# Two banded mixing layers: which engine scales two of the eight columns of the second norm, and which copies the band's products

## The chip, the cores and the metric

The kernel runs on one core of one Trainium2 chip. The core has five engines that run side by side, each through its own list of instructions in order: TensorE (PE in the profile; its weight loads are PEld), VectorE (DVE), ScalarE (ACT), GpSimd (POOL) and SyncE (SP), which here issues the loop's transfers. The metric is the time of one execution on the device in microseconds (us).

## The reference

The input x is 512 x 512 x 64 in float32. Two layers follow one another, each `x = x + layer(gn(x))`, with this body (H = 128, window 4):

```
xn    = ln(gn(x))                                     # 64 channels
left  = (xn @ Wl + bl) * mask * sigmoid(xn @ Wlg + blg)   # 128 channels
right = (xn @ Wr + br) * mask * sigmoid(xn @ Wrg + brg)
gate  = sigmoid(xn @ Wog + bog)
band[i, j, :] = sum over |d| <= 4 of left[i + d, i, :] * right[i + d, j, :]
out   = (ln(band) * out_norm_scale + out_norm_bias) * gate
y     = out @ Wo + bo                                 # back to 64 channels
```

`ln` takes mean and variance over the channels of one position. The second norm, the one meant in the title, is `ln(band)`: 128 channels per position.

## The kernel before

Rows of x come in 9 blocks of 64 rows that overlap by the window, and the columns in two halves that lie on the partitions: partition e*64 + i is row i of the block, half e. Half a row, 256 columns, is worked through in 2 chunks of 128 columns, each in 16 units of 8 columns. That makes 9 x 2 x 16 = 288 units per layer, and as many outputs.

The loop in `layer` runs over steps t. One step works on one unit coming in and, some 30 steps behind it, on one output going out:

- In: `scaled` and `moved` (the affine of the group norm, z times ga plus gb), `inner_stats`, `centred`, `rescaled` (the first norm), `transposed`, `kept` (the transposed unit, zT, also written to the DRAM tensor `later`), `right` (the projections, into two PSUM banks), `right_gate` (sigmoid, sg), `right_end` (the product into RO). The four elementwise steps on z run on GpSimd, apart from the first units of each layer, which VectorE scales and moves.
- Between: `mix` multiplies a slab of the left factors, A, with RO: the band's products for 8 channels and a whole chunk, in two PSUM banks. Two copies, "copy a" and "copy b", put them back into RO in place of the right factors. Each chunk has 16 such products, spread over ten of its 16 steps as 2, 1, 2, 2, 1, 2, 1, 2, 2, 1, and none in the other six.
- Out: `out_stats` (statistics of RO, sto), `norm` (the second norm of the 8 columns of one output, one instruction per column, from RO into the tile `on`), `turned` (transposes of `on`), `gates` and `gated`, `times_gate` (ZH), `end` (the product with Wo), `ended` (the addition to x, in XR) and, in the first layer, `sums` and `biased`.

Every fourth step, `solve` computes the reciprocal roots for both norms at once: `prepare` on ScalarE ("solve on a") and thirteen small instructions on VectorE, `roots` ("solve on d"). They leave rs and nm, the factor and the offset of each column.

What stands where is written out by hand: FIRST and SECOND list the parts of one step for the two layers, and each engine gets its instructions in the order of that list. `keep_in_program_order` (line 381) holds every instruction of the loop to it, so nearly all rows of the profile name that line, and the tile names tell them apart. The tile `on` has one buffer: the columns of the next output are written only when `turned` has read this one.

Of the 8 columns of an output, GpSimd scales the last `nv` ("norm columns"; 1 in the first layer, 2 in the second) and ScalarE the others, columns 0 to 3 early in the step and the rest at its end. `copy a` is ScalarE's. `copy b` is VectorE's, apart from the second product of a step in the first layer, which is ScalarE's.

Of the kernel before, what the change touches and what calls it, by code (L numbers as in the profile page):

```python
# [10 lines left out]
AF = mybir.ActivationFunctionType  # L11
ALU = mybir.AluOpType
# [10 lines left out]
JU = 8  # L23
# [9 lines left out]

APART = (False, True)
NV = (1, 2)
SECOND_ON_ACT = (True, False)

FIRST = [
    ("out stats", 2), "gates", "gated", ("project", 0), ("project", 4), "turn",
    ("sigmoid", 0), ("out stats", 3), "scale", ("right", 0), ("sigmoid", 4),  # L40
    ("norm", (0, 4)), "norm columns", "centre", "move", "last product", ("right", 4),
    "times gate", "rescale", "transpose", ("out stats", 99), "inner stats", "keep", "solve",
    "end", ("band", 0), ("copy a", 0), "sums", "bias", ("band", 1), ("copy b", 0),
    ("solve on", "a"), "scale next", "move next", ("norm", (4, 8)), ("copy a", 1),
    ("solve on", "d"), ("copy b", 1),
]
# [2 lines left out]
    ("sigmoid", 0), ("project", 4), ("out stats", 99), ("right", 0), ("sigmoid", 4), "turn",  # L49
    ("norm", (0, 4)), "last product", "norm columns", "centre", "scale next", "rescale",  # L50
    "times gate", "transpose", ("band", 0), "keep", "move next", "end", ("right", 4),
    ("copy b", 0), "inner stats", "solve", "move", ("copy a", 0), ("band", 1),
    ("solve on", "a"), ("copy b", 1), ("copy a", 1), ("norm", (4, 8)), ("solve on", "d"),
]
ORDERS = (FIRST, SECOND)
# [48 lines left out]
def tile_two_banded_layers(  # L104
# [9 lines left out]
    x, out = x[0], out[0]  # L114
# [268 lines left out]
    class en:  # L383
        tensor, vector, scalar, gpsimd, sync = map(
            InOrder, (nc.tensor, nc.vector, nc.scalar, nc.gpsimd, nc.sync)
        )
# [285 lines left out]

        return {"a": [prepare], "d": [roots]}

    def norm(o: Out, lo: int, hi: int, pool: bool):
        if lo == 0:
            o.on = onp.tile([P, JU, H], F32, tag="on", name="on")
        for j in range(lo, hi):
            to, of = o.on[:, j, :].rearrange("p (h t) -> p h t", t=2), RO[:, :, o.c + j, :]
            rs, nm = o.rs[:, j : j + 1], o.nm[:, j : j + 1]  # L680
            if pool:
                en.gpsimd.tensor_scalar(to, of, rs, nm, ALU.mult, ALU.add)
            else:
                en.scalar.activation(to, of, AF.Identity, bias=nm, scale=rs)

    def recall(o: Out):
        o.t = ztg.tile([P, JU // 2, P], F32, tag="zg", name="zg")
# [96 lines left out]
    def layer(src: bass.AP, dst: bass.AP, w: dict, stats: bool, then=None):  # L784
# [4 lines left out]
        units, outs, lefts, mixes, looks, slabs = {}, {}, {}, {}, {}, {}  # L789
# [4 lines left out]
        for c in range(n_chunks):  # L794
            b, t0 = blocks[c // per], (c + 1) * NU
            for k in range(NU):
                t = c * NU + k
# [4 lines left out]
            for f in range(NU):  # L802
                o = outs[c * NU + LAG + f] = Out(
                    b, units[c * NU + (f + own) % NU], c % per * JC + f * JU
                )
# [10 lines left out]
        for n in range(0, NEAR * JQ, JU):  # L816
            t = 3 + n // JU * 2
# [24 lines left out]
            load(src, u)  # L842
        yield
        A, sti, sto = {}, {}, None
        order, nv, second_on_act = (x[0 if stats else 1] for x in (ORDERS, NV, SECOND_ON_ACT))
        for t in range(min(loads), last_t + 3):
            if then and t == max(units) + 2:
                then()
            if t + 3 in outs:
                recall(outs[t + 3])  # L850
            for u in loads.get(t, []):
                if u not in early:
                    load(src, u)
            if t + 1 in outs:
                fetch(src, outs[t + 1], w, t + 1)
            for c, h in slabs.get(t, []):
                A[c, h] = take_left(c // per, h)

            looking = []
            for o, k in looks.get(t, []):  # L860
                if sto is None:
                    sto = sm.tile([P, NB // 2, 6], F32, tag="sto", name="sto"), []
                st, os = sto
                if k == 0:
                    os.append(o)
                n = (len(os) - 1) * (JU // 2)
                looking.append((o, st[:, n : n + JU // 2, :], k))
            todo = []
            for at, u in inners.get(t, []):
                key = (at + 1) // 4  # L870
                if key not in sti:
                    sti[key] = sm.tile([P, 3 * NB // 4, 6], F32, tag="sti", name="sti", bufs=3), []
                st, us = sti[key]
                n = len(us) * (JU // 2)
                u.mean = st[:, n : n + JU // 2, 1::3]
                todo += [(u, st[:, n : n + JU // 2, :], k) for k in range(JU // 2)]
                us.append(u)
            mixing, mixed, solving = mixes.get(t, []), [], {}
            now, later_on = affines.pop(t, []), []
            if t % 4 == 0 and t > NU:  # L880
                later_on = affines.pop(t + 1, [])
            if t in lefts:
                for q in range(0, min(JU, NEAR * JQ - lefts[t].near), JQ):
                    left(lefts[t], q, w)
            which = lambda u: en.vector if u.at < NU + 4 else en.gpsimd

            for item in order:
                name, n = item if isinstance(item, tuple) else (item, None)
                u, o, p = units.get(t), outs.get(t), outs.get(t - 1)
                if name == "out stats":  # L890
                    for v in looking[:n]:
                        out_stats(*v)
                    looking = looking[n:]
                elif name == "scale":
                    for v in now:
                        scaled(v, which(v))
                elif name == "move":
                    for v in now:
                        moved(v, which(v))
                elif name == "scale next":  # L900
                    for v in later_on:
                        scaled(v, en.gpsimd)
                elif name == "move next":
                    for v in later_on:
                        moved(v, en.gpsimd)
                elif name == "project" and u:
                    right(u, n, w)
                elif name == "sigmoid" and u:
                    right_gate(u, n)
                elif name == "right" and u:  # L910
                    right_end(u, n)
                elif name == "gates" and o:
                    gates(o, w)
                elif name == "gated" and o:
                    gated(o)
                elif name == "turn" and o:
                    turned(o, w)
                elif name == "times gate" and o:
                    times_gate(o, w)
                elif name == "centre":  # L920
                    for v in inputs(t + 2):
                        centred(v)
                elif name == "rescale":
                    for v in inputs(t + 2):
                        rescaled(v)
                elif name == "transpose":
                    for v in inputs(t + 1):
                        transposed(v)
                elif name == "keep":
                    for v in inputs(t + 1):  # L930
                        kept(v)
                elif name == "bias" and o:
                    biased(o, w)
                elif name == "inner stats":
                    for v in todo:
                        inner_stats(*v)
                elif name == "last product" and p:
                    end(p, w)
                elif name == "end" and p:
                    ended(dst, p)  # L940
                elif name == "sums" and t - 2 in outs:
                    sums(outs[t - 2], t - 2 == first_t, t - 2 == last_t)
                elif name == "solve" and t % 4 == 0:
                    st, us = sti.pop((t + 4) // 4, (None, []))
                    so, os = sto or (None, [])
                    sto = None
                    if us or os:
                        solving = solve(w, us, os, st, so)
                elif name == "solve on":
                    for f in solving.pop(n, []):  # L950
                        f()
                elif name == "norm" and t + 1 in outs:
                    lo, hi = n
                    norm(outs[t + 1], lo, min(hi, JU - nv), False)
                elif name == "norm columns" and t + 1 in outs:
                    norm(outs[t + 1], JU - nv, JU, True)
                elif name == "band" and len(mixing) > n:
                    c, h0 = mixing[n]
                    mixed.append(mix(c, A[c, h0 // HA], h0, stats))
                elif name == "copy a" and len(mixing) > n:  # L960
                    en.scalar.copy(*mixed[n][0])
                elif name == "copy b" and len(mixing) > n:
                    (en.scalar.copy if n and second_on_act else en.vector.tensor_copy)(*mixed[n][1])

    class Slices:

# [143 lines left out]
```

## Time and profile before

| | |
|---|---|
| time, median of 3 runs | 4660.42 us (4649.69 to 4669.49) |
| span of the profiled execution, first to last instruction | 4644.6 us |
| TensorE busy | 3860.9 us, 83% of the span |
| VectorE busy | 3999.6 us, 86% |
| ScalarE busy | 3596.2 us, 77% |
| GpSimd busy | 3278.3 us, 71% |
| the second norm's columns on ScalarE | 3744 instructions, 492 ns each |
| the same on GpSimd | 864 instructions, 451 ns each |

The page gives the profiled execution's span; the time of a run lies a little above a span, 16 us here between the median and this one. The first layer's loop runs from about 260 us to 2470 us, the second's from there to the end, so the shares of the span are means over two loops, their beginnings and ends, and the statistics of the input ahead of them. A busy TensorE is not TensorE at its peak. In a row of grouped instructions, the first number behind the bar is the time that at least one of them ran, the next the mean length of one; instructions of an engine overlap a little, so the first may be less than number times length. Behind the second bar stands the idle time just before them and what ended it.

### The profile page before, as it was taken

To read this page: it belongs to the slowest core of one execution; us is meant where nothing else is said; L and a number is where in the kernel's file an instruction comes from. 1 tells how busy PE (TensorE), PEld (TensorE's weight loads), DVE (VectorE), ACT (ScalarE), POOL (GpSimd) and SP (SyncE) were. 2 spreads that over 40 slices of the span, in tenths; PEclk is the share of its full clock that TensorE was granted. 3 is DMA by queue.
4 is the path that set the end of the run, shared out by engine and by line. 5 is a ranking of instruction groups with operands and counts; after the bars stand their busy time and mean duration, and the time that the engine had idled before them with its cause. 6 is when DMAs were issued, how large, how long until landed. Compare 5 with 4: busy or idle time off the path is not lost. (4 is left out here: it accounts for less than half of the span.)

```text
span 4644.6 us, 192669 instructions
## 1 busy us (share of the span) xinstructions
PE 3860.9 (83%) x76306; PEld 3310.7 (71%) x76306; DVE 3999.6 (86%) x10943; ACT 3596.2 (77%) x8410; POOL 3278.3 (71%) x3427
## 2 busy tenths in 40 slices
PE   1024899999999999999984389899999898899998
PEld 0023788888888888888863378777777787778776
DVE  7954798898899989899876379999999999999998
ACT  0012799999999999999983268888888888888888
POOL 0034888888888888888733387877778777778751
PEclk9986999999999999999997699999999999999999
DMA  7949678777878777888763968888888888888876
GB/s 309 394 134 99 177 218 221 218 218 219 222 220 222 217 219 217 225 220 224 211 184 95 72 191 219 222 223 224 221 227 221 226 226 225 222 222 223 227 210 184
DMA packets 1437803, 983.43 MB, mean 212 GB/s; under 512 B 167362, under 2 KB 1284584, under 8 KB 1432552
## 3 DMA queue, kind: packets, MB, share of 16 engines
q1 hardware_dynamic: 1432064, 969.69, 77.1%
q8 instruction: 603, 9.88, 0.9%
q14 instruction: 296, 2.42, 0.2%
q10 hardware_dynamic: 4840, 1.43, 0.1%
HBM read 658.35 MB, written 312.40 MB: 209 GB/s over the span
## 5 line engine op out<-in xcount | busy, mean ns | idle before, releaser
L381 ACT ACTIVATE on<-RO,nm,rs 128x128 f32<-128x128 f32 x3744 | 1589.4, 492 | 87.7 <-DVE nm L381 50.8
L381 PEld LDWEIGHTS banks<-pack,zT 64*128 64x128 f32 x18576 | 1270.1, 197 | 467.4 <-ACT zT L381 324.5
L381 PE MATMUL banks<-pack,zT 64*128 64x128 f32 x18576 | 1326.1, 287 | 262.2 <-ACT zT L381 234.8
L381 DVE TENSOR_TENSOR RO<-banks,sg 128x512 f32<-128x512 f32 (+1 forms) x1188 | 794.6, 676 | 306.9 <-ACT sg L381 206.1
L381 ACT ACTIVATE sg<-banks 128x512 f32<-128x512 f32 (+1 forms) x1188 | 694.1, 591 | 254.9 <-PE banks L381 227.3
L381 POOL TENSOR_TENSOR z<-z,ga 128x512 f32<-128x512 f32 x536 | 682.0, 1281 | 184.5 <-DMA z<-mid_x 169.5
L381 DVE BATCH_NORM_STATS2 sto<-RO 128x6 f32<-128x256 f32 x2304 | 803.3, 412 | 0.8
L381 POOL TENSOR_SCALAR on<-RO,rs,nm 128x128 f32<-128x128 f32 x864 | 384.2, 451 | 566.3 <-ACT sg L381 309.8
L381 DVE SCALAR_TENSOR_TENSOR ZH<-bank,pack,gate 128x448 f32<-128x448 f32 (+1 forms) x1152 | 739.1, 683 | 43.7 <-ACT gate L381 24.8
L381 PE MATMUL bank<-zg,pack 64*128 64x448 f32 (+1 forms) x2304 | 724.8, 595 | 19.0 <-ACT RO L381 8.3
L381 PE MATMUL bank<-pack,ZH 128*64 128x64 f32 x18432 | 669.4, 226 | 21.4 <-DVE nm L381 20.5
L381 POOL TENSOR_TENSOR z<-z,gb 128x512 f32<-128x512 f32 x536 | 678.0, 1278 | 5.1
L381 POOL TENSOR_TENSOR z<-z,rs 128x512 f32<-128x512 f32 x586 | 618.5, 1056 | 72.3 <-DVE rs L381 45.4
L381 POOL TENSOR_TENSOR z<-z,sti 128x512 f32<-128x512 f32 x586 | 624.9, 1067 | 21.4 <-DVE sti L381 21.4
L381 PEld LDWEIGHTS bank<-pack,ZH 128*64 128x64 f32 x18432 | 589.6, 139 | 64.6 <-DVE nm L381 27.5
L381 ACT ACTIVATE zT<-banks 128x512 f32<-128x512 f32 (+1 forms) x1084 | 461.9, 477 | 146.0 <-DMA later<-zT 75.3
L381 ACT ACTIVATE gate<-bank 128x448 f32<-128x448 f32 (+1 forms) x1152 | 562.5, 540 | 5.8 <-PE bank L381 2.7
L381 DVE BATCH_NORM_STATS2 sti<-z 128x6 f32<-128x128 f32 x2344 | 503.7, 282 | 1.4 <-POOL z L381 1.2
L381 PE MATMUL bank<-ident,on 64*128 64x64 f32 x9216 | 459.5, 226 | 31.1 <-ACT gate L381 28.3
L381 PEld LDWEIGHTS bank<-ident,on 64*128 64x128 f32 x9216 | 429.3, 141 | 74.9 <-ACT gate L381 50.2
L381 DVE TENSOR_TENSOR XR<-bank,XR 120x512 f32<-120x512 f32 (+1 forms) x576 | 390.9, 679 | 5.2 <-POOL XR L381 2.3
L381 PE MATMUL banks<-ident,z 64*128 64x64 f32 x4336 | 251.1, 234 | 131.2 <-DVE RO L381 68.7
(154 smaller groups left out, 4025.2 us busy)
## 6 DMA issues: line engine op xcount, KB each, us to landing
later<-zT SPq DMA_DIRECT2D x576, 256.0 KB
A<-left_of SPq DMA_DIRECT2D x1152, 128.0 KB
zg<-later SPq DMA_DIRECT2D x576, 256.0 KB
z<-in_x_dram SPq DMA_DIRECT2D x576, 128.0 KB
z<-mid_x SPq DMA_DIRECT2D x576, 128.0 KB
gn_x<-in_x_dram SPq DMA_DIRECT2D x16, 4096.0 KB
XR<-in_x_dram SPq DMA_DIRECT2D x448, 112.0 KB
mid_x<-XR SPq DMA_DIRECT2D x448, 112.0 KB
```

The lines of the kernel that those rows point to most:

```text
L381: return lambda *a, **k: tc.keep_in_program_order(f(*a, **k))
```

## The change

Columns 8 - nv - 2 and the one after it are scaled on VectorE, as one `tensor_scalar` each, in a new part of the step called "norm vector". ScalarE keeps 5 of the 8 columns in the first layer and 4 in the second; GpSimd keeps its own. All copies of the band's products are on ScalarE, and in the second layer "copy b" of the first product moves in the list from ahead of the inner statistics to behind "copy a".

```
+DVE_NORM = 2
 FIRST = [
...
-    "end", ("band", 0), ("copy a", 0), "sums", "bias", ("band", 1), ("copy b", 0),
+    "end", ("band", 0), ("copy a", 0), "sums", "norm vector", "bias", ("band", 1),
+    ("copy b", 0),
...
 SECOND = [
...
-    ("copy b", 0), "inner stats", "solve", "move", ("copy a", 0), ("band", 1),
+    "inner stats", "norm vector", "solve", "move", ("copy a", 0), ("copy b", 0), ("band", 1),
...
-            if pool:
-                en.gpsimd.tensor_scalar(to, of, rs, nm, ALU.mult, ALU.add)
+            if engine is en.scalar:
+                engine.activation(to, of, AF.Identity, bias=nm, scale=rs)
             else:
-                en.scalar.activation(to, of, AF.Identity, bias=nm, scale=rs)
+                engine.tensor_scalar(to, of, rs, nm, ALU.mult, ALU.add)
...
-                    norm(outs[t + 1], lo, min(hi, JU - nv), False)
+                    norm(outs[t + 1], lo, min(hi, JU - nv - DVE_NORM), en.scalar)
...
+                elif name == "norm vector" and t + 1 in outs:
+                    norm(outs[t + 1], JU - nv - DVE_NORM, JU - nv, en.vector)
...
-                    (en.scalar.copy if n and second_on_act else en.vector.tensor_copy)(*mixed[n][1])
+                    en.scalar.copy(*mixed[n][1])
```

The lists of TensorE, GpSimd and SyncE stay as they are; only VectorE's and ScalarE's change. VectorE's list in the middle of the first layer, a step with one product of the band, before (sti and sto are the statistics of the two norms):

```order
L381 BN_STATS sti<-z 128x6 x4
L381 TENSOR_TENSOR XR_977<-bank,XR_977 120x4x128
L381 COPY RO<-banks 128x2x256
L381 BN_STATS sto<-RO 128x6 x4
L381 TENSOR_TENSOR RO<-banks,sg 128x64x8 x2
```

The same step with the change:

```order
L382 BN_STATS sti<-z 128x6 x4
L382 TENSOR_TENSOR XR_977<-bank,XR_977 120x4x128
L382 TENSOR_SCALAR on<-RO,rs,nm 128x128 x2
L382 BN_STATS sto<-RO 128x6 x4
L382 TENSOR_TENSOR RO<-banks,sg 128x64x8 x2
```

The copy out of the PSUM banks is gone, and two columns of the norm stand in its place, in steps without a product too.

ScalarE's list in the second layer, a solving step with two products of the band, before (var and the two rows behind it are `prepare`):

```order
L381 ACTIVATE zT<-banks 128x4x64
L381 COPY RO<-bank 128x2x256
L381 ACTIVATE var<-sti,ln_eps 128x32
L381 COPY bank<-sto 128x32
L381 ACTIVATE bank<-sto 128x32
L381 COPY RO<-bank 128x2x256
L381 ACTIVATE on<-RO,nm,rs 128x128 x2
L381 ACTIVATE gate<-bank 128x448 x2
```

The same step with the change:

```order
L382 ACTIVATE zT<-banks 128x4x64
L382 COPY RO<-bank 128x2x256 x2
L382 ACTIVATE var<-sti,ln_eps 128x32
L382 COPY bank<-sto 128x32
L382 ACTIVATE bank<-sto 128x32
L382 COPY RO<-bank 128x2x256 x2
L382 ACTIVATE gate<-bank 128x448 x2
```

`prepare` now stands behind two copies of the first product instead of one, two copies follow it instead of one, and the two late columns of the norm are gone from ScalarE.

More of the change, by code (lines that the diff above doesn't have):

```diff
@@ L35 @@
 NV = (1, 2)
-SECOND_ON_ACT = (True, False)
+DVE_NORM = 2
 FIRST = [
@@ L673, in solve, with norm @@
         return {"a": [prepare], "d": [roots]}
-    def norm(o: Out, lo: int, hi: int, pool: bool):
+    def norm(o: Out, lo: int, hi: int, engine):
         if lo == 0:
@@ L844, in layer @@
         A, sti, sto = {}, {}, None
-        order, nv, second_on_act = (x[0 if stats else 1] for x in (ORDERS, NV, SECOND_ON_ACT))
+        order, nv = (x[0 if stats else 1] for x in (ORDERS, NV))
         for t in range(min(loads), last_t + 3):
@@ L953, in layer @@
                     lo, hi = n
-                    norm(outs[t + 1], lo, min(hi, JU - nv), False)
+                    norm(outs[t + 1], lo, min(hi, JU - nv - DVE_NORM), en.scalar)
                 elif name == "norm columns" and t + 1 in outs:
-                    norm(outs[t + 1], JU - nv, JU, True)
+                    norm(outs[t + 1], JU - nv, JU, en.gpsimd)
+                elif name == "norm vector" and t + 1 in outs:
+                    norm(outs[t + 1], JU - nv - DVE_NORM, JU - nv, en.vector)
                 elif name == "band" and len(mixing) > n:
```

## The prediction

> **What bounds the kernel now.** I read the busy time by stretch first, for the steady middle of each layer; columns after the window's length are PE, PEld, DVE, ACT and POOL busy us.
>
> ```profile
> 929.00:2322.00 1393.00, 1344.33 (x28011) 1169.66 (x28006) 1254.61 (x3402) 1290.14 (x3035) 1204.85 (x1186) 1.00 0.80 220
> 2786.00:4528.00 1742.00, 1585.42 (x31584) 1369.81 (x31580) 1636.27 (x4436) 1509.08 (x3503) 1343.83 (x1502) 0.98 0.81 223
> ```
>
> To turn these into steps I took the groups of instructions of the same two stretches, the first layer's here: one GpSimd column per step, so 201 steps of 1393/201 = 6.93 us.
>
> ```profile
> L381 ACT ACTIVATE on<-RO,nm,rs 128x128 f32<-128x128 f32 x1409 | 596.9, 492 | 13.9 <-DVE nm L381 11.2 <-POOL z L381 1.4 <-ACT sg L381 0.5
> L381 POOL TENSOR_SCALAR on<-RO,rs,nm 128x128 f32<-128x128 f32 x201 | 90.6, 451 | 135.6 <-ACT sg L381 89.3 <-PE bank L381 44.6
> L381 DVE COPY RO<-banks 128x512 f32<-128x512 f32 x124 | 84.6, 683 | 0.7 <-ACT RO L381 0.7
> ```
>
> In the second layer two GpSimd columns per step, so 256 steps of 1742/256 = 6.80 us:
>
> ```profile
> L381 DVE BATCH_NORM_STATS2 sto<-RO 128x6 f32<-128x256 f32 x1024 | 355.2, 411 | 0.1
> L381 POOL TENSOR_SCALAR on<-RO,rs,nm 128x128 f32<-128x128 f32 x512 | 226.2, 452 | 215.5 <-ACT sg L381 186.0 <-PE bank L381 27.4
> L381 DVE BATCH_NORM_STATS2 sti<-z 128x6 f32<-128x128 f32 x988 | 212.0, 282 | 1.4 <-POOL z L381 1.2
> L381 DVE COPY RO<-bank 128x512 f32<-128x512 f32 x257 | 175.4, 682 | 10.0 <-PE bank L381 8.8
> L381 ACT COPY RO<-bank 128x512 f32<-128x512 f32 x257 | 150.1, 585 | 39.2 <-PE bank L381 37.7
> ```
>
> Per step that is, in us: first layer PE 6.69, ACT 6.42, DVE 1254.61/201 = 6.24, POOL 5.99; second layer DVE 1636.27/256 = 6.39, PE 6.19, ACT 5.89, POOL 5.25. Four engines are nearly full. In the first layer PE leads at 97% with DVE at 90%; in the second DVE leads at 94%. So an extra half microsecond of DVE work per step cannot be hidden in either layer. The waits of the second layer show the rest of its step:
>
> ```profile
> POOL z L381 <- DMA z<-mid_x: 162.5, 47, 6.1
> PEld banks L381 <- ACT zT L381: 138.7, 96, 5.3
> DVE bank L381 <- ACT bank L381: 37.5, 17, 4.9
> ```
>
> Some is data arriving late (162.5 us); the third row is DVE waiting for ScalarE's preparation of the reciprocal roots.
>
> **The change, part by part.**
>
> ScalarE loses two columns per step, 2 x 596.9/1409 = 0.85 us. It gains the copies that VectorE made: 124/201 = 0.62 per step in the first layer and one per step in the second, at 150.1/257 = 0.58 us. Net -0.49 and -0.26 us per step. ScalarE does not lead in either layer, so I give this no gain of its own; its cover is DVE.
>
> VectorE loses the same copies: 84.6/201 = -0.42 us per step in the first layer, 175.4/256 = -0.69 in the second. It gains two columns per step, 128 elements from RO in SBUF to `on` in SBUF with two per-partition scalars. No such VectorE instruction runs in the loop now. The nearest rows are in the set-up, SBUF to SBUF with one per-partition scalar:
>
> ```profile
> L247 DVE TENSOR_SCALAR aug<-raw,ns 128x640 f32<-128x640 f32 x2 | 1.1, 544 | 17.2 <-DMA nb<-in_L_conv_norm_bias_dram 17.2
> L245 DVE TENSOR_SCALAR hb<-half,nb 128x128 f32<-128x128 f32 x2 | 0.6, 278 | 0.0
> ```
>
> So 0.278 us each by the row of the same size. As instructions overlap their neighbours' ends, the floor is the 128-element statistics, 212.0/988 = 0.215 us each. I take 0.50 us for the pair. Were that all, DVE would go to 6.24 + 0.50 - 0.42 = 6.32 and 6.39 + 0.50 - 0.69 = 6.20: even, and slightly lighter.
>
> It is not all. The two set-up rows differ by 512 elements and 266 ns, 0.52 ns an element; the two statistics rows differ by 128 elements and 129 ns, 1.01 ns an element. VectorE's SBUF-to-SBUF scalar operation therefore takes two elements at a time and must read SBUF over two paths. What happens when VectorE reads SBUF over two paths while GpSimd works is in this trace, at the start of the second layer, where VectorE does some units' affine step itself (z and ga or gb both in SBUF). Undisturbed, then beside GpSimd (columns: start us, length us):
>
> ```profile
> 2499.58 1.28 DVE L381 TENSOR_TENSOR z<-z,ga 128x512 f32<-128x512 f32 x2
> 2620.24 0.95 DVE L381 TENSOR_TENSOR z<-z,gb 128x512 f32<-128x512 f32 x1
> 2621.11 1.52 DVE L381 TENSOR_TENSOR z<-z,ga 128x512 f32<-128x512 f32 x1
> 2619.59 1.05 POOL L381 TENSOR_TENSOR z<-z,sti 128x512 f32<-128x512 f32 x1
> 2620.72 1.37 POOL L381 TENSOR_TENSOR z<-z,rs 128x512 f32<-128x512 f32 x1
> ```
>
> Alone, two take 1.28 us, 0.6 to 0.7 each. Beside GpSimd the first ends at 2621.19, 0.55 us after GpSimd's ends at 2620.64; GpSimd's next is stretched from its usual 1.05 to 1.37 us behind it; and VectorE's second, issued at once, ends at 2622.63, 0.54 us after that one's end at 2622.09. They take strict turns, whole instruction by whole instruction, and a second VectorE instruction has to let a waiting GpSimd instruction pass. The other VectorE work of the loop reads one operand from PSUM or has only one; the new pair would be the loop's first to collide.
>
> Where the pair stands, GpSimd is in the middle of its list. One step of the first layer, where the pair would follow the XR row:
>
> ```profile
> 1512.14 0.68 DVE L381 TENSOR_TENSOR XR<-bank,XR 120x512 f32<-120x512 f32 x1
> 1512.73 1.72 DVE L381 BATCH_NORM_STATS2 sto<-RO 128x6 f32<-128x256 f32 x5
> 1512.10 1.04 POOL L381 TENSOR_TENSOR z<-z,rs 128x512 f32<-128x512 f32 x1
> 1513.10 1.18 POOL L381 TENSOR_TENSOR XR<-XR,fewer 120x512 f32<-120x512 f32 x1
> ```
>
> The first column would wait from 1512.8 to 1513.14, the second until after the 1.18 us behind it. On average: GpSimd's share is 1204.85/1393 = 0.865 with 1204.85/1186 = 1.02 us an instruction, and 1343.83/1742 = 0.771 with 1343.83/1502 = 0.89. The first of the pair waits share x half an instruction, 0.44 and 0.35 us; the second share x a whole one, 0.88 and 0.69. Together 1.32 and 1.04 us per step of VectorE standing still in order, with the inner products, the gates and the statistics behind it, and PE behind those for its PSUM banks. Bounds of this term: 0 if a one-input instruction with two scalars reads over one path, and 2 x 1.02 and 2 x 0.89 if every column meets a whole instruction.
>
> The Trainium skill, page "SBUF — State Buffer", section "Who interferes with whom", says that a `tensor_scalar` in VectorE's two-port mode and a GpSimd instruction exclude each other for the whole instruction, whichever came first. By that rule the sum comes to the 5080 us below, and by the instructions' own lengths alone to the 4591 us of the first rival. The trace agrees with turns for the two-input form (0.55 and 0.54 us after GpSimd's end), and no run here shows them yet for `tensor_scalar`.
>
> GpSimd loses about 0.15 us to each column (half of a 0.278), 0.3 us per step: 6.3 and 5.55, under DVE's new total and so hidden.
>
> Two waits move. `turn` on PE now also waits for VectorE's pair; it stands a step later behind the gates and projections, so 0, or the pair's own delay where VectorE is late, which the sum has. ScalarE's preparation of the roots now stands behind a second copy: +0.58 us on each of the 288/4 = 72 solves per layer; covered by VectorE, whose pair sits ahead of the roots, and 2 x 72 x 0.58 = 84 us if uncovered.
>
> **The sum.** VectorE per step: 6.24 + 1.32 + 0.50 - 0.42 = 7.64, and 6.39 + 1.04 + 0.50 - 0.69 = 7.24 us. PE falls to 6.69/7.64 = 88% and 85% beside it, so VectorE alone leads, with a wider margin than now. At 98% busy the step is 7.80 and 7.39, +0.87 and +0.59 us. Over 288 steps per layer: 251 + 170 = 421 us. The profiled execution spans 4644.6 us; the median of the runs, 4660.4, lies 16 us above it. So 4644.6 + 421 + 16 = 5082, **about 5080 us**. With VectorE at 100%: (0.71 + 0.44) x 288 = 331, 4992; at today's 94%: (1.20 + 0.90) x 288 = 605, 5265.
>
> **Rivals.**
>
> No collision: the strided rows of RO keep the instruction on one path, or `tensor_scalar` does not exclude GpSimd. For it: no row shows a scalar operation beside GpSimd; against it: 0.52 ns an element. The first layer stays bound by PE (idle 0.24 us per step; perhaps 0.05 gained), the second gains up to 6.39 - 6.20 = 0.19: (0.05 + 0.19) x 288 = 69, 4591 us. It decides from the point where the pair costs VectorE less than the copies, 0.42 and 0.69 us.
>
> One wait per pair: VectorE runs both columns in one turn. The second wait goes: 6.76 and 6.55, under today's 6.93 and 6.80. The latencies of the full engines remain, some 0.1 us per step: 4690 us. Against it: the second instruction above was overtaken.
>
> The roots come late: no collision, but the 84 us uncovered: 4591 + 84 = 4675. For it: the 37.5 us row; against it: two columns fewer ahead on ScalarE.
>
> **How the numbers follow.** Turns for both columns 0.78; no collision 0.13; one wait 0.06; late roots 0.03. The likeliest gives the time; its own range is 4900 to 5340, the top from 2.0 us of waiting in the first layer and 1.8 in the second at 98%: (1.57 + 1.37) x 288 would be 847, 5500; half way to that is 5290, and the 94% end of the likeliest adds some 50. The range starts at 4680, to hold one wait per pair, and leaves out the case without collision. A measurement of this kernel can tell about 0.5%, 23 us, from no change: faster 0.12, same 0.05 (parts of the last two), slower 0.83.
>
> **What would show it.** Right: VectorE's `on` rows well over 0.278 us on average, with a mean near (1.32 + 0.50)/2 = 0.9 us and a minimum near 0.25; GpSimd's z rows above their 1.04 to 1.28; VectorE's share at 97% or more, PE's under 90% in the first layer's middle (6.69 of 6.93 us, 97%, now); ScalarE's `on` rows 2592 in number (1440 + 1152) and under 70% busy. Wrong: `on` rows on VectorE at 0.2 to 0.3 us throughout; then the time falls or stays, and the second layer's step shows it. If the rows are long but the time is near 4700, the waits fell where VectorE was idle anyway.

## The result, and the profile after

The kernel with the change takes 4936.4 us (median of 4 runs, 4928.0 to 4949.6) against 4665.0 us for the kernel before (4 runs, 4649.7 to 4670.5): a ratio of 1.0595, 95% interval 1.0574 to 1.0615. It is slower by 271 us, where 415 to 420 us were forecast. The profiled execution spans 4947.6 us, its own time being 4949.6 us.

The busy times of the whole execution, from the page:

```profile
PE 3983.6 (81%) x76306; PEld 3390.6 (69%) x76306; DVE 4429.2 (90%) x11627; ACT 3469.6 (70%) x7726; POOL 3278.5 (66%) x3427
```

VectorE went from 3999.6 to 4429.2 us, and every other engine's share fell. TensorE was nevertheless busy for longer, 3983.6 us against 3860.9, while its granted clock over the span was 0.941 against 0.959; what part of the loss goes with the clock was not separated. The groups of instructions of the whole execution show which rows carry it (behind the bar: us busy, mean ns of one):

```profile
L382 DVE TENSOR_SCALAR on<-RO,rs,nm 128x128 f32<-128x128 f32 x1152 | 793.8, 729 | 0.0
...
L382 POOL TENSOR_TENSOR z<-z,ga 128x512 f32<-128x512 f32 x536 | 681.8, 1280 | 39.6 <-DMA z<-mid_x 28.0 <-DMA z<-in_x_dram 11.6
...
L382 POOL TENSOR_TENSOR z<-z,rs 128x512 f32<-128x512 f32 x586 | 618.8, 1057 | 72.4 <-DVE rs L382 45.5
...
L382 POOL TENSOR_SCALAR on<-RO,rs,nm 128x128 f32<-128x128 f32 x864 | 383.8, 451 | 1071.1 <-ACT sg L382 364.0 <-DVE nm L382 277.6 <-PE bank L382 268.4
```

Two of these rows before, for comparison:

```profile
L381 POOL TENSOR_TENSOR z<-z,ga 128x512 f32<-128x512 f32 x536 | 682.0, 1281 | 184.5 <-DMA z<-mid_x 169.5 <-DMA z<-in_x_dram 9.7 <-PE bank L381 4.0
...
L381 POOL TENSOR_SCALAR on<-RO,rs,nm 128x128 f32<-128x128 f32 x864 | 384.2, 451 | 566.3 <-ACT sg L381 309.8 <-PE bank L381 211.2 <-DVE nm L381 30.9
```

A column on VectorE lasts 729 ns on average, and the instructions of the tile `on` (minimum, median, maximum in ns) show that its length is not steady:

```profile
L382 ACT ACTIVATE on<-RO,nm,rs x2592: 476/489/537, 532.7 to 4939.1; 128x128 f32<-128x128 f32 x200
L382 DVE TENSOR_SCALAR on<-RO,rs,nm x1152: 319/492/3271, 535.6 to 4940.0; 128x128 f32<-128x128 f32 x192
L382 POOL TENSOR_SCALAR on<-RO,rs,nm x864: 438/449/474, 532.9 to 4938.5; 128x128 f32<-128x128 f32 x173
```

ScalarE and GpSimd need the same time for every column, 476 to 537 and 438 to 474 ns. VectorE's range from 319 to 3271. What lies between them is in the timeline of the first layer: a step in which GpSimd has nothing to do, then one in which it has (start us, length us).

```profile
1309.87 0.60 DVE L382 TENSOR_SCALAR on<-RO,rs,nm 128x128 f32<-128x128 f32 x2
...
1312.91 0.45 POOL L382 TENSOR_SCALAR on<-RO,rs,nm 128x128 f32<-128x128 f32 x1 [3.42 <-ACT sg L382]
...
1316.20 1.66 DVE L382 TENSOR_SCALAR on<-RO,rs,nm 128x128 f32<-128x128 f32 x2
1317.78 0.41 DVE L382 BATCH_NORM_STATS2 sto<-RO 128x6 f32<-128x256 f32 x1
1315.59 1.04 POOL L382 TENSOR_TENSOR z<-z,rs 128x512 f32<-128x512 f32 x1
1316.59 1.18 POOL L382 TENSOR_TENSOR XR<-XR,fewer 120x512 f32<-120x512 f32 x1
```

Alone, while GpSimd stands idle for the 3.42 us before 1312.91, the pair takes 0.60 us. Beside GpSimd the pair takes 1.66 us and ends at 1317.86, 0.09 us after GpSimd's second instruction ends at 1317.77; the statistics behind it start only then. In the second layer the same, with two instructions of 1.25 us:

```profile
3761.64 2.55 DVE L382 TENSOR_SCALAR on<-RO,rs,nm 128x128 f32<-128x128 f32 x2
3764.11 0.41 DVE L382 BATCH_NORM_STATS2 sto<-RO 128x6 f32<-128x256 f32 x1
3761.61 2.50 POOL L382 TENSOR_TENSOR z<-z,ga 128x512 f32<-128x512 f32 x2
```

What these two steps show holds throughout, as the start and end of every instruction in the trace give it. Of the 1152 columns, 606 last longer than 0.36 us, and each of the 606 ends 0.080 to 0.092 us after the end of an instruction of GpSimd. In 279 of the 576 pairs the first column waits (it lasts over 0.45 us). In 190 of them GpSimd's next instruction began within 0.06 us, and the second column waited for that one too; in the other 89 it did not, and the second column did not wait. Among the first columns, 48 waited for the ends of two GpSimd instructions, having started less than 0.15 us before the first of these ends. Three, the longest at 3.26 to 3.27 us, waited for three, though they had started 0.73 us before the first; why is open.

The stretches in the middle of each layer give the step (PE, PEld, DVE, ACT, POOL busy us), with the pair's rows in the same stretches, the first layer's ahead of the second's:

```profile
929.00:2322.00 1393.00, 1280.45 (x26179) 1104.89 (x26176) 1345.68 (x3464) 1153.96 (x2573) 1147.57 (x1125) 0.99 0.75 206
3100.00:4750.00 1650.00, 1437.41 (x27409) 1232.92 (x27410) 1598.26 (x4094) 1274.39 (x2819) 1190.08 (x1324) 0.95 0.75 205
```

```profile
L382 DVE TENSOR_SCALAR on<-RO,rs,nm 128x128 f32<-128x128 f32 x373 | 274.4, 775 | 0.0
L382 POOL TENSOR_SCALAR on<-RO,rs,nm 128x128 f32<-128x128 f32 x187 | 84.4, 451 | 235.1 <-ACT sg L382 73.1 <-PE bank L382 65.4 <-DVE nm L382 47.5
...
L382 DVE TENSOR_SCALAR on<-RO,rs,nm 128x128 f32<-128x128 f32 x444 | 332.7, 789 | 0.0
L382 POOL TENSOR_SCALAR on<-RO,rs,nm 128x128 f32<-128x128 f32 x442 | 194.9, 451 | 426.6 <-ACT sg L382 209.8 <-DVE nm L382 131.2 <-PE bank L382 63.8
```

187 and 442/2 = 221 steps: 7.45 and 7.47 us a step, where 6.93 and 6.80 were. VectorE is busy 1345.68/187 = 7.20 and 1598.26/221 = 7.23 us of it, 97% in both layers. The pair costs 274.4 x 2/373 = 1.47 and 332.7 x 2/444 = 1.50 us a step, of which 0.60 is what it needs alone and 0.87 and 0.90 are waiting.

### The profile page after: what moved, and what is told of

Read it like the earlier page. It is cut to its first block, busy times and chain, and to the rows that moved or that the text cites. A ratio compares the mean times of both kernels' runs of the same rounds, so it can differ in the third digit from the quotient of the medians.

```text
span 4947.6 us, 192786 instructions
## 1 busy us (share of the span) xinstructions
PE 3983.6 (81%) x76306; PEld 3390.6 (69%) x76306; DVE 4429.2 (90%) x11627; ACT 3469.6 (70%) x7726; POOL 3278.5 (66%) x3427
## 4 chain that ended last, share of the span: by engine, by line
PE 40%; DVE 35%; issue 8%; DMA 8%; POOL 5%; SPq 3%; ACT 2%; ACTq 0%; DVEq 0%; POOLq 0%
PE bank L382 19%; PE banks L382 18%; DVE on L382 6%; DVE RO L382 4%; DVE sto L382 4%; DVE ZH L382 4%; POOL z L382 3%; DVE sti L382 3%; SPq L382 3%; PE acc L382 3%; DVE bank L382 2%; DVE XR L382 2%; DVE gn_st L382 2%; DVE rsqrt_u L382 2%; DVE rsqrt_t L382 1%
## 5 line engine op out<-in xcount | busy, mean ns | idle before, releaser
L382 PEld LDWEIGHTS banks<-pack,zT 64*128 64x128 f32 x18576 | 1288.4, 198 | 402.0 <-ACT zT L382 251.3
L382 PE MATMUL banks<-pack,zT 64*128 64x128 f32 x18576 | 1346.0, 287 | 207.7 <-ACT zT L382 187.9
L382 ACT ACTIVATE on<-RO,nm,rs 128x128 f32<-128x128 f32 x2592 | 1109.6, 492 | 271.1 <-DVE nm L382 220.8
L382 DVE TENSOR_TENSOR RO<-banks,sg 128x512 f32<-128x512 f32 (+1 forms) x1188 | 777.6, 670 | 247.7 <-ACT sg L382 147.1
L382 PE MATMUL bank<-zg,pack 64*128 64x448 f32 (+1 forms) x2304 | 774.5, 617 | 25.0 <-DVE ZH L382 14.5
L382 DVE TENSOR_SCALAR on<-RO,rs,nm 128x128 f32<-128x128 f32 x1152 | 793.8, 729 | 0.0
L382 POOL TENSOR_TENSOR z<-z,ga 128x512 f32<-128x512 f32 x536 | 681.8, 1280 | 39.6 <-DMA z<-mid_x 28.0
L382 POOL TENSOR_TENSOR z<-z,gb 128x512 f32<-128x512 f32 x536 | 676.9, 1277 | 5.1
L382 POOL TENSOR_TENSOR z<-z,rs 128x512 f32<-128x512 f32 x586 | 618.8, 1057 | 72.4 <-DVE rs L382 45.5
L382 ACT ACTIVATE gate<-bank 128x448 f32<-128x448 f32 (+1 forms) x1152 | 583.1, 550 | 93.4 <-PE bank L382 65.3
L382 POOL TENSOR_TENSOR z<-z,sti 128x512 f32<-128x512 f32 x586 | 625.1, 1067 | 21.0 <-DVE sti L382 21.0
L382 PE MATMUL bank<-ident,on 64*128 64x64 f32 x9216 | 484.3, 227 | 37.5 <-ACT gate L382 20.8
L382 PEld LDWEIGHTS bank<-ident,on 64*128 64x128 f32 x9216 | 445.6, 140 | 90.3 <-ACT gate L382 42.4
```

The source lines that it names most:

```text
L382: return lambda *a, **k: tc.keep_in_program_order(f(*a, **k))
```

## The experiments

All times below are set against runs of the kernel before on the same chip, 4656 to 4661 us.

**The two halves of the change.** First the copies alone:

```
-DVE_NORM = 2
+DVE_NORM = 0
```

> Half of the change: all copies on ScalarE, and all eight columns where they were. Theory A (VectorE's pair of columns waits for GpSimd): without the pair there is nothing to wait for; VectorE falls to about 6.24 - 0.42 = 5.8 and 6.39 - 0.69 = 5.7 us a step, ScalarE rises to 6.42 + 0.36 = 6.8 and 5.89 + 0.58 = 6.5; the time stays near that of before, 4650 to 4760 us. Theory B (the copies are the cost: two on ScalarE in series hold the PSUM banks longer and bring the roots late): about as slow as the change, 4880 us or more.

Measured: 4667.1 us, ratio 1.0021 (1.0007 to 1.0035). On ScalarE the copies cost next to nothing, and theory B falls. What they did to the engines shows in the stretches of this run:

```profile
929.00:2322.00 1393.00, 1344.71 (x27886) 1172.68 (x27886) 1172.69 (x3270) 1325.37 (x3141) 1201.98 (x1182) 1.00 0.80 219
2786.00:4528.00 1742.00, 1605.95 (x31506) 1388.32 (x31500) 1485.12 (x4176) 1593.52 (x3750) 1356.72 (x1512) 0.97 0.82 223
```

In the second layer VectorE's share fell from 94% (1636.27 us of this stretch) to 85%, ScalarE's rose from 87% to 91%, and the time stayed. So work taken off VectorE and given to ScalarE gains nothing. Whether VectorE had not held the layer, or ScalarE holds it now in its place, this run cannot tell.

Then the two columns alone, with the copies where they had been:

```
+SECOND_ON_ACT = (True, False)
...
-    "inner stats", "norm vector", "solve", "move", ("copy a", 0), ("copy b", 0), ("band", 1),
+    ("copy b", 0), "inner stats", "norm vector", "solve", "move", ("copy a", 0), ("band", 1),
...
-                    en.scalar.copy(*mixed[n][1])
+                    (en.scalar.copy if n and second_on_act else en.vector.tensor_copy)(*mixed[n][1])
```

> The other half: two columns on VectorE, the copies where they were. Theory A: the copies' VectorE time is not given back, so VectorE goes to 6.24 + 1.4 = 7.6 and 6.39 + 1.4 = 7.8 us a step and the time to about 5200 us (5100 to 5300), slower than the whole change. Theory B: near the time of before, 4600 to 4720 us.

Measured: 5248.9 us, ratio 1.1255 (1.1227 to 1.1283), as theory A had it. It is 313 us slower than the whole change. The copies given back to VectorE, 0.42 and 0.69 us a step over 288 steps each, make 320 us: once VectorE leads, its time counts one for one.

**Odd and even counts.** Each VectorE column was cut in two, once unevenly and once evenly:

```
+            elif engine is en.vector:
+                for part in (slice(0, 33), slice(33, H // 2)):
+                    engine.tensor_scalar(to[:, part], of[:, part], rs, nm, ALU.mult, ALU.add)
             else:
                 engine.tensor_scalar(to, of, rs, nm, ALU.mult, ALU.add)
```

(33 stands for the uneven cut; the even one has 32 in its place.)

> The change with each VectorE column cut into 33 and 31 pairs of channels, so that the rows read are an odd number and the elements written an even one. Theory A with two paths: an odd count cannot be halved between two paths, so the four instructions read one element at a time, take no turns with GpSimd, run 0.2 to 0.25 us each and need about 0.6 us a step; the time falls back to 4600 to 4720 us. Theory A without two paths (any VectorE instruction from SBUF to SBUF with two scalars waits): four waits instead of two, 5000 us or more. Theory B: as the change, 4900 to 4960 us.

> As the run with 33 and 31, but cut into 32 and 32 pairs, even counts: the same four instructions a step. Theory A: each may take a turn with GpSimd, so some 2.0 to 2.6 us a step instead of 1.4, and the time is 5100 to 5400 us. Theory B, or a cost of the number of instructions: the same as the run with 33 and 31.

Measured: with 33 and 31 pairs of channels 4765.7 us, ratio 1.0224 (1.0205 to 1.0243); with 32 and 32 pairs 5384.7 us, ratio 1.1552 (1.1523 to 1.1581). The same four instructions on the same data differ by 619 us only in how the column is cut, into odd or even counts of pairs. A pair is two neighbouring channels in RO, so the uneven cut reads 33 or 31 rows of two elements and writes one run of 66 or 62. The columns' rows, first of the uneven cut, minimum, median and maximum in ns:

```profile
L382 DVE TENSOR_SCALAR on<-RO,rs,nm x2304: 312/330/351, 538.2 to 4760.9; 128x66 f32<-128x66 f32 x192
```

and of the even one:

```profile
L382 DVE TENSOR_SCALAR on<-RO,rs,nm x2304: 286/308/1417, 534.1 to 5373.5; 128x64 f32<-128x64 f32 x192
```

With odd counts no instruction waits: 2304 of them lie between 312 and 351 ns, and 1212 of these started while an instruction of GpSimd had at least 0.25 us still to run. With even counts the shortest is shorter, 286 ns, and the longest lasts 1417; each of the 846 above 0.34 us ends 0.046 to 0.056 us after an instruction of GpSimd. So the even form has to wait for GpSimd, and the odd form does not. From the first instruction's start to the last one's end, the four take 1.07 us a step on average in the uneven cut, and 2.27 and 2.04 us in the even one (first and second layer, worked out from the start and end of each instruction in the traces; the change's pair by the same count 1.37 and 1.39). The time follows: the even cut adds (0.90 + 0.65) x 288 = 446 us to the change by that count and 448 by the clock; the uneven one takes off (0.30 + 0.32) x 288 = 179 and 171.

The forecast of 4600 to 4720 us for the uneven cut was missed by 46 us, since the four take 1.07 us a step where 0.6 had been expected: the four start 0.25 us after one another, though each is half a column.

**One instruction per column without turns.** VectorE scaled 63 of the 64 pairs of channels in one instruction, and another engine the last pair; the first run with ScalarE, the second with GpSimd (`en.gpsimd.tensor_scalar` in place of the activation below):

```
+            elif engine is en.vector:
+                engine.tensor_scalar(to[:, :63], of[:, :63], rs, nm, ALU.mult, ALU.add)
+            elif engine is None:
+                en.scalar.activation(to[:, 63:], of[:, 63:], AF.Identity, bias=nm, scale=rs)
...
                     norm(outs[t + 1], JU - nv, JU, en.gpsimd)
+                    norm(outs[t + 1], JU - nv - DVE_NORM, JU - nv, None)
```

> Each VectorE column in one instruction over 63 of the 64 pairs of channels (an odd count, so one path and no turns); ScalarE scales the last pair, two small instructions a step. Theory A: VectorE's set takes about 0.7 us a step (1.07 measured for four short ones, less two fixed parts), 6.5 and 6.4 us a step in all, ScalarE 6.35 and 6.04; the time goes below the 4766 us of the run with 33 and 31, to 4570 to 4690 us, where TensorE holds it. Rival: the number of instructions is what counts and the odd count was not the cause; then the two long instructions wait as in the change, about 4930 us.

> As the run before, with the last pair on GpSimd beside its own columns. GpSimd's price for two elements is between 0.1 us and the 0.45 us of a whole column, so it rises from 6.1 and 5.4 to 6.3 to 7.0 and 5.6 to 6.3 us a step. Theory A: 4570 to 4700 us, the upper end if GpSimd becomes the leader of the first layer. Rival as for the run before: about 4930 us.

Measured: 4755.5 us with ScalarE, ratio 1.0206 (1.0186 to 1.0226); 4682.9 us with GpSimd, ratio 1.0049 (1.0030 to 1.0068). The rows of the columns, of the run with ScalarE:

```profile
L382 DVE TENSOR_SCALAR on<-RO,rs,nm 128x126 f32<-128x126 f32 x1152 | 406.6, 395 | 0.0
...
L382 ACT ACTIVATE on<-RO,nm,rs 128x2 f32<-128x2 f32 x1152 | 376.8, 375 | 0.0
```

and, VectorE's row being the same there, of the run with GpSimd:

```profile
L382 POOL TENSOR_SCALAR on<-RO,rs,nm 128x2 f32<-128x2 f32 x1152 | 385.3, 347 | 0.0
```

VectorE's instructions do not wait here either (none lasts over 416 ns in either run), and 2 x 406.6/1152 = 0.71 us a step is the price of two columns without turns, half of the change's. The run with ScalarE misses its forecast of 4570 to 4690 us by 65. Two elements cost ScalarE 375 ns where 0.21 us had been reckoned, and giving them to GpSimd instead is worth 73 us; as ScalarE was busy for 92% of the first layer's middle, the same share as VectorE and under TensorE's 95%, it was not full, and the way from its longer work to the time is not shown. The run with GpSimd lies in its range of 4570 to 4700 us, at the upper end, which had been tied to GpSimd leading the first layer: it was busy for 1331.72 of that layer's 1393 us, 96%, as much as TensorE. So two columns on VectorE without turns bring the time back to that of before, and no lower.

**One column instead of two.**

```
-DVE_NORM = 2
+DVE_NORM = 1
```

> One whole column on VectorE instead of two, uncut, so it takes turns with GpSimd; ScalarE has one column more. Theory A: one wait of about 0.4 us and 0.33 us of work, 0.73 a step instead of 1.38; VectorE 6.24 + 0.73 - 0.42 = 6.55 and 6.44 us a step; 4580 to 4700 us. If the waits come in the second column only (after a first has let GpSimd pass), the column takes 0.35 to 0.6 us and the time is at the lower end. Rival, that VectorE's time is not what counts: half of the change's loss, about 4800 us.

Measured: 4680.6 us, ratio 1.0043 (1.0027 to 1.0059). The column lasts 643 ns on average:

```profile
L382 DVE TENSOR_SCALAR on<-RO,rs,nm 128x128 f32<-128x128 f32 x576 | 370.3, 643 | 0.0
```

With 0.33 us alone it waits some 0.3 us, and most of the loss is gone: VectorE's sum, 6.24 + 0.64 - 0.42 = 6.46 and 6.39 + 0.64 - 0.69 = 6.34 us a step, is about that of before. The time lies in the range of theory A, and the rival's 4800 us falls.

**What holds the time once VectorE is light.** The kernel with the copies on ScalarE and no VectorE column, with two instructions of the roots' chain left out:

```
             vec.scalar_tensor_tensor(y, u, 5.0, y, add, mult)
-            vec.tensor_tensor(u, y, v, mult)
-            vec.tensor_tensor(t, y, u, mult)
```

> What holds the time near 4660 us once VectorE is light: the kernel with all copies on ScalarE and no VectorE column, and two of the thirteen instructions of the roots' chain left out (the second iteration uses the first one's product, so the scale of both norms is off). Theory C, the chain of the solve every fourth step is what the other engines wait for: 144 solves x 2 x 0.26 us = 75 us faster than that kernel, about 4590 us. Theory D, TensorE and ScalarE hold the steps and the solve is hidden or caught up later: no more than 20 us faster, 4645 us or more.

(A solve for both norms has fourteen instructions on VectorE in the trace, not thirteen.)

Measured: 4651.4 us, ratio 0.9986 (0.9971 to 1.0001), against 1.0021 with the whole chain: 16 us of the 75. The chain is mostly hidden; theory D holds as far as this goes. Which of the other engines' waits makes the floor near 4660 us was not separated.

**Another place.** The pair taken from its place in both lists and put directly behind GpSimd's columns:

```
-    ("norm", (0, 4)), "norm columns", "centre", "move", "last product", ("right", 4),
+    ("norm", (0, 4)), "norm columns", "norm vector", "centre", "move", "last product", ("right", 4),
...
-    "end", ("band", 0), ("copy a", 0), "sums", "norm vector", "bias", ("band", 1),
+    "end", ("band", 0), ("copy a", 0), "sums", "bias", ("band", 1),
...
-    ("norm", (0, 4)), "last product", "norm columns", "centre", "scale next", "rescale",
+    ("norm", (0, 4)), "last product", "norm columns", "norm vector", "centre", "scale next", "rescale",
...
-    "inner stats", "norm vector", "solve", "move", ("copy a", 0), ("copy b", 0), ("band", 1),
+    "inner stats", "solve", "move", ("copy a", 0), ("copy b", 0), ("band", 1),
```

> The change with the pair moved in the list to directly behind GpSimd's own columns, so that VectorE reaches it while GpSimd is at its short column instruction (0.45 us) or still waiting. If the waits are a matter of chance against GpSimd's share, the pair takes 1.3 to 1.5 us as in the change, and the time is 4900 to 5000 us. If the place decides, the first column waits less than 0.3 us and the second meets one 1.06 us instruction at most, a pair of 0.9 to 1.3 us; the time is 4700 to 4900 us, less what VectorE loses by waiting there for the transposes.

Measured: 5053.8 us, ratio 1.0847 (1.0823 to 1.0870). The columns themselves wait less, 544 ns on average instead of 729:

```profile
L382 DVE TENSOR_SCALAR on<-RO,rs,nm 128x128 f32<-128x128 f32 x1152 | 579.2, 544 | 77.2 <-PE bank L382 48.8 <-ACT gate L382 9.1 <-POOL z L382 0.4
```

So the place decides how much of GpSimd's work the pair meets: from the first start to the last end it takes 1.00 and 1.01 us on average in the two layers, within the 0.9 to 1.3 expected. But the pair now waits for TensorE's transposes (48.8 us) with VectorE's product into RO queued behind it, and that product's wait for the sigmoid, as the waits of the run have it, is larger than in the change:

```profile
DVE RO L382 <- ACT sg L382: 358.9, 299, 10.0
```

In the change it was 147.1 us:

```profile
L382 DVE TENSOR_TENSOR RO<-banks,sg 128x512 f32<-128x512 f32 (+1 forms) x1188 | 777.6, 670 | 247.7 <-ACT sg L382 147.1
```

The columns gain 2 x 0.185 us a step, 213 us over 576 steps; the two waits cost 77 + 212 = 289 us more than in the change. That accounts for 76 of the 117 us by which this run is slower. The rest was not traced: VectorE is only 87% busy in the first layer's middle here, and TensorE's granted clock over the span is 0.902, against 0.941 in the change. Both expectations had the time too low.

## Why the prediction was right, point by point

- **VectorE's scalar operation takes two elements at a time and so takes turns with GpSimd: right, and shown.** It was argued from a slope of two set-up rows and from another form of instruction. The odd and even counts show it for this form: no wait in 2304 instructions against instructions of up to 1417 ns. The lengths show the two elements: with even counts, 64 elements more (128 against 64) add 319 - 286 = 33 ns to the shortest, 0.52 ns an element; with odd counts, 62 more (126 against 64 on average) add 395 - 330 = 65 ns, 1.05 an element. The Trainium skill, page "VectorE: DVE Perf Modes", section "The perf-mode tier table", gives `tensor_scalar` in fp32 from SBUF twice the rate of `tensor_tensor`; the traces agree that the even form has twice the rate of the odd one. The Trainium skill, page "SBUF — State Buffer", section "Who interferes with whom", states that a `tensor_scalar` in the two-port mode and a GpSimd instruction exclude each other; these runs show it on VectorE's side.
- **Strict turns, in which a second VectorE instruction lets GpSimd pass: right, but for three columns.** In all 190 pairs in which the first column had waited and GpSimd's next instruction followed at once, the second waited as well. The rival of one wait per pair falls. The three columns that three GpSimd instructions delayed do not fit.
- **The wait, 1.32 and 1.04 us a step: mis-sized.** It measured 0.87 and 0.90. This is the term that failed, in the first layer above all. By columns, taking 0.34 us off each as the mean length of one that does not wait, the first column waited 0.26 and 0.39 us where 0.44 and 0.35 had been reckoned, the second 0.61 and 0.51 where 0.88 and 0.69. The forecast took GpSimd's share of the steps before, 0.865 and 0.771, and pairs that come at random. GpSimd's share fell with the longer step, to 1147.57/1393 = 0.82 and 1190.08/1650 = 0.72, and its idle time lies largely in one piece, ahead of its own columns (566 us before the change, 1071 after), where part of the pairs meet nobody: in 177 of the 576 neither column lasts over 0.45 us. How much of the shortfall each of these makes was not separated. The run in another place shows that the place moves the wait, from 729 ns a column to 544.
- **The pair alone, 0.50 us: 0.60.** Where neither column waits, the second starts 0.253 us behind the first and the last lasts its full 0.34 us; the forecast had 0.25 for each and nothing for the overhang. What sets these lengths was not tested.
- **VectorE's sum and share.** By the sum with the measured pair, 6.24 + 1.47 - 0.42 = 7.29 and 6.39 + 1.50 - 0.69 = 7.20; measured 7.20 and 7.23. The forecast had 7.64 and 7.24; that the second layer came so close is partly luck, since a wait 0.14 us too long met a pair 0.10 us too short. The 98% forecast for its share came out as 97%. With 7.45 and 7.47 us a step, the loss is (0.52 + 0.67) x 288 = 343 us by the middles of the layers, and 303 between the two profiled spans; what the beginnings and ends of the layers do differently is open.
- **GpSimd's rows above their lengths: wrong.** They are 1280, 1277, 1067 and 1057 ns for the four steps on z, and were 1281, 1278, 1067 and 1056 before. The 0.15 us taken for each column does not show in them.
- **The copies, covered by ScalarE: right.** 4667 us with them alone. The late roots as a rival fall with it.
- **The other signs.** ScalarE's `on` rows number 2592, as forecast. VectorE's shortest is 319 ns and the mean 729, where 0.25 and 0.9 us had been named. TensorE's share in the first layer's middle is 1280.45/1393 = 92%, not under 90%, and ScalarE's 70% of the span, not under it.
- **The rival without collision, 4591 us: too low.** Without turns, the two columns give 4683 us, in a kernel in which VectorE needs 0.71 us for them, not 0.50, and GpSimd two small instructions of 0.35 us more a step. VectorE's sum was taken as what holds the second layer, from its 94%. With the copies alone its share fell to 85% and the time stayed, while ScalarE's rose to 91%. So the gain reckoned from VectorE's sum alone did not come; which engine or wait holds the second layer then is open.

## What to carry to other kernels

When work moves to VectorE, ask not only how long it takes there but what it shares. In this kernel a `tensor_scalar` from SBUF to SBUF over an even count (128 or 64 elements) ran two elements at a time and had to wait for whole GpSimd instructions, up to several times its own length. Read as an odd number of rows of two (63, 33 or 31) and written as one run, it did not wait at all; other odd shapes were not tried. What a wait costs also depends on the place in VectorE's list, with all that is queued behind it. Once VectorE led, what was added to it counted one for one (313 us measured, 320 reckoned). Taking work off it gained nothing when ScalarE got that work: no variant that computes the same result was faster than the kernel before.

## What the runs showed of the hardware that had not been expected

- In the change, the turns show on one side only: GpSimd's instructions kept their length to a few ns (1067 and 1057 ns for the two steps of the first norm, 1067 and 1056 before) while VectorE's columns went from 0.34 to 0.73 us. It is not so everywhere: with the pair directly behind GpSimd's own columns, these lasted 491 ns on average instead of 451, and up to 779.
- Cutting a column into odd counts is cheaper than leaving it whole and even: four instructions without turns take 1.07 us a step, two with turns 1.37.
- Two elements cost ScalarE 375 ns and GpSimd 347 ns, against 492 and 451 ns for 128: most of the time of these short instructions does not go with the number of elements.
